# Layer 2's first products on half their channels, an operand made in two steps, and statistics moved to later slots

## The chip, the cores and the metric

The kernel runs on one core of a Trainium2 chip. The metric is the device time of one execution in microseconds, lower is better; the median of three executions before the change is 2750.5 us. One core has a matrix engine (TensorE, "PE" in the profile, with its weight loads as "PEld"), a vector engine (VectorE, "DVE"), an activation engine (ScalarE, "ACT"), a general engine (GpSimd, "POOL") and a queue for transfers (SyncE, "SP"). [...]

## What is computed

An image x of 1024 channels and 64 x 64 pixels goes through four layers, each as x + layer(groupnorm32(x)). Layer 0 mixes rows by a decay matrix. Layers 1 and 3 are products with a 1024 x 1024 matrix over the channels. Layer 2 is a selective scan:

```python
xz = silu(einsum('oc,bchw->bohw', in_proj_w, x) + in_proj_b)
x_ssm, res, gate = split(xz, 3, axis=1)
xf = silu(depthwise_conv3(x_ssm) + dw_b)
dbc = einsum('oc,bcn->bon', dbc_w, xf) + dbc_b
# dt, B, C and xf are gathered in a permuted order of pixels
y_h = selective_scan(x_h, dt, A, B_t, C_t, Dparam)
# and y is brought back to the order of the image
y = y_h * silu(gate) + res
return silu(einsum('oc,bchw->bohw', out_proj_w, y) + out_proj_b)

x = x + L0(gn(x)); x = x + L1(gn(x)); x = x + L2(gn(x)); x = x + L3(gn(x))
```

## The kernel before

**Products.** The pixels are cut in eight blocks nb of 512, taken as four pairs. The 1024 x 1024 products of layer 1 (W1) and of layer 2's x_ssm and res (WX, WR) are done on a pair at a time by a scheme of seven products for a 2 x 2 block product. `b_sets` makes a pair's operand tiles in steps: b21, b11 and b22 are normed quarters of the image (`make`, an activation on ScalarE, L921), t1 is such a quarter less b11, t2 = b22 - t1, t3 = t2 - b11, t4 = b21 - t2 (subtractions, L790). Each name has four tiles of 128 x 512, one for each k (KH = 4). t1's subtractions are on VectorE; those of t2, t3, t4 on GpSimd, except t2 in a stage's first pair and all of them in WX's last pair. A step ends at each `yield`.

`multiply` issues seven products for each half g of the output channels (NG = 2), so fourteen for a pair, in the order b21, b11, b22, t2, t3, t1, t4 (called p1 to p7 here, p8 to p14 for the second half). A product is two output tiles o times four k, eight matmuls of 128 x 512 (L835), each of which the trace shows as two records. Two pairs of accumulator banks alternate; after a product, `put` copies or adds its result and `add` adds to it (layer 1: on VectorE, L936 and L940, into the image in place; WX: `put2a` L1081 copies on ScalarE to xs and `add2a` L1089 adds on VectorE; WR: rg, L997 and L1001).

`run` goes over the pairs. While a pair is multiplied, the next pair's first five steps are taken, one after each of the last five products, and the rest (`late`) after the first products of its own pair.

**Order of the work.** Around these stages the order on PE, DVE, ACT and POOL is that in which the program writes the instructions; only SP's list is set by a planner. So what stands ahead of what is read from the code and from the trace.

**The border of layers 1 and 2.** The loop over layer 1's products takes the group norm's statistics for layer 2 in two halves of the channels: FIRST, the channels of the first half g, and SECOND. `norm_steps` turns them into a bias and a scale: a matmul over groups (pg, L198), three small vector operations (L201 to L203), a second matmul (pv, L207), and `rsqrt` with two activations and three vector operations. For FIRST (gn2a) this runs beside layer 1's last products. Behind the loop two activations make b21[0] and b21[1], whose channels are in FIRST. `multiply` with `begun` takes p1's k = 0, 1 for both outputs and then k = 2, 3; after the first half it yields, SECOND's statistics (gn2b) are finished, and five steps of the set are taken.

**With the scan (WR).** The scan over the permuted tokens goes on between half products: a gather from DRAM (L1237, on POOL), a turn on PE (pr, L1251 and L1252), decays on DVE (L1258 to L1266), pg on PE (L1273), E and its sum on DVE (L1281, L1283), G (L1286), y as a matmul with G (py, L1290), its copies on ACT (L1293, L1295) and a scatter to DRAM (L1299, on POOL). Behind WX a loop of its own (from L1211) does the last convolutions: `follow` turns finished tiles (L1057), convolves (L1035, L1038) and applies a Silu (L1109); between, half products of WR's first pair are issued.

**Gate, out_proj and layer 3** go by the same scheme on two levels, 49 slots a job (`two_steps`, matmul L1641, operands L1405 and L1409). A job of the kind "out" adds the image to its four result tiles by an accumulating DMA from GpSimd (`take_image`), takes their statistics on VectorE (`quarter_stats`, L1448) and stores the tiles (`keep`); what each needs is put on a list of slots by `on(slot, ...)`. The statistics of a pair's last tiles (Q and D) fall into the first slots of the next pair's gate job, beside the subtractions for its own operands (qt, L1405).

Of the kernel before, what the change touches and what calls it, by code (L numbers as in the profile page):

```python
# [18 lines left out]
P = 128  # L19
# [25 lines left out]
KH = CT // 2  # L45
# [45 lines left out]
def tile_net(ctx: ExitStack, tc: tile.TileContext, x, par_d, cst_d, w_d, w2_d, dbcw_d, out):  # L91
# [684 lines left out]

    def b_sets(B, make, first=False, eng=None):

        def plain(name, row, col):
            B.setdefault(name, [])  # L780
            for k in range(len(B[name]), KH):
                t = b_tile(name, k, B["name"])
                make(t, row * KH + k, col)
                B[name].append(t)

        def comb(name, one, two, ks, eng):
            if name not in B:
                B[name] = [b_tile(name, k, B["name"]) for k in range(KH)]
            for k in ks:
                eng.tensor_tensor(B[name][k], B[one][k], B[two][k], ALU.subtract)  # L790

        slow = nc.vector if first else eng or nc.gpsimd
        plain("b21", 1, 0)
        yield
        plain("b11", 0, 0)
        yield
        plain("b22", 1, 1)
        yield
        plain("t1", 0, 1)
        comb("t1", "t1", "b11", range(KH), nc.vector)  # L800
        yield
        comb("t2", "b22", "t1", range(KH), slow)
# [14 lines left out]
    def multiply(m, B, put, add, fine=False, begun=False):  # L817

        for g in range(NG):
            one, two = ("A", "B") if turn_[0] == 0 else ("B", "A")
            turn_[0] ^= 1

            def banks(tag, what):
                return [gemm[-1].tile([P, FB], F32, tag=tag, name=f"mm{what}_{m}_{B['name']}_{g}_{i}")
                        for i in range(OG)]

            def product(to, i, name, fresh):
                w = weights(m, g, i)  # L830
                split = begun and g == 0 and i == 1
                for j in range(2):
                    for o, ks in ((0, range(2 * j, 2 * j + 2)), (1, range(2 * j, 2 * j + 2))) if split else ((j, range(KH)),):
                        for k in ks:
                            nc.tensor.matmul(to[o], w[:, k, o * P : (o + 1) * P], B[name][k],  # L835
                                             start=(fresh and k == 0), stop=(k == KH - 1),
                                             skip_group_check=True)
                    if fine and j == 0:
                        yield True

            def out(fn, row, col, ps):
                for o in range(OG):
                    fn(row * KH + g * OG + o, col, ps[o])

            b = banks(two, 2)
            yield from product(b, 1, "b21", True)
            out(put, 0, 0, b)
            yield
            a = banks(one, 1)
            yield from product(a, 0, "b11", True)  # L850
            out(add, 0, 0, a)
            yield
            b = banks(two, 3)
            yield from product(b, 6, "b22", True)
            out(put, 0, 1, b)
            yield
            yield from product(a, 4, "t2", False)
            out(put, 1, 0, a)
            yield
            b = banks(two, 7)  # L860
            yield from product(b, 5, "t3", True)
            out(put, 1, 1, b)
# [11 lines left out]
    def run(pairs, mats, make, put, add, before=None, after=None, last_eng=None, fine=False, tell=False, B=None, begun=None):  # L874

        def sets(i):
            B = begun if begun and i == 0 else {"name": f"{mats[0]}_{pairs[i]}"}  # L880

            def steps():
                if before is not None:
                    before(pairs[i])
                yield from b_sets(B, lambda t, ct, col: make(t, ct, 2 * pairs[i] + col), first=(i == 0),
                                  eng=last_eng if i == len(pairs) - 1 else None)
            return B, steps()


        if B is None:  # L890
            B, steps = sets(0)
            for _ in range(5 if begun is None else 0):
                next(steps)
        else:
            steps = iter(())
        for i, pair in enumerate(pairs):
            late = steps
            nxt, steps = sets(i + 1) if i + 1 < len(pairs) else (None, iter(()))
            left = 7 * NG * len(mats)
            for m in mats:  # L900
                for half in multiply(m, B, lambda o, c, ps: put(m, o, 2 * pair + c, ps),
                                     lambda o, c, ps: add(m, o, 2 * pair + c, ps), fine, begun and i == 0):
                    if half:
                        yield True
                        if B is begun and "b11" not in B:
                            for _ in range(5):
                                next(late)
                        continue
                    if tell:
                        yield False  # L910
                    left -= 1
                    next(steps if left < 5 else late, None)
# [52 lines left out]
    with tc.manual_schedule(engines={E_.DVE, E_.PE, E_.Pool, E_.Activation}):  # L965
        for i, _ in enumerate(pointwise("l1", W1, "b1", [3, 2] + EARLY, x0_d, x1_d)):
            busy = next(sums, None) if i % 14 < 13 else None
            sort_on(not busy, (0, 0, 0, 0, 3, 2, 1, 2, 1, 3, 3, 3, 0, 0)[i % 14])
            if i == last - 6:
                chain = norm_steps("gn2a", *moments("gn2a", FIRST), len(FIRST), finer=True)  # L970
            elif last - 6 < i < last - 1:
                next(chain)
            elif i == last - 1:
                columns(FIRST, finish_of(chain), norm2)
                mv2 = moments("gn2b", SECOND, range(2))
        for _ in sums:
# [35 lines left out]
    with tc.tile_pool(name="l2a", bufs=2) as pa, tc.tile_pool(name="l2a2", bufs=1) as pa2, \  # L1012
# [68 lines left out]
            nc.scalar.copy(xs[o][:, 2 + side * FB : 2 + (side + 1) * FB], ps)  # L1081

        CONVS = 2
        have, ready, due, due2, due3 = set(), [], [], [], []

        def add2a(m, o, nb, ps):
            pair, side = divmod(nb, 2)
# [11 lines left out]
        def follow():  # L1099


            for c in due3:
                turn(*c)
            made = [conv(*c) for c in due]
            due3[:] = due2
            due2[:] = []
            for o, nb, ps in made:
                cv = pa.tile([P, FB], F32, tag="cv", name=f"cv{o}_{nb}", bufs=4)
                nc.scalar.activation(cv, ps, AF.Silu)  # L1109
                due2.append((o, nb, cv))  # L1110
            due[:] = ready[:CONVS]
            del ready[:CONVS]

        def finish(pair):
            n = 2 * TPB
# [55 lines left out]
        with tc.manual_schedule(engines={E_.DVE, E_.PE, E_.Pool, E_.Activation}):  # L1171
            nc.sync.dma_start(both[:, :, P:], dbcw_d)
            nc.gpsimd.tensor_copy(both[:, :, :P], ident.unsqueeze(1).to_broadcast([P, CT, P]))
            nc.gpsimd.memset(row, 0.0)
            ends, i = iter(()), -1
# [196 lines left out]
    def two_steps(jobs, norm2):  # L1372
# [96 lines left out]
        def plan(j):  # L1469
# [89 lines left out]
            for name, row, col, when in done:  # L1559
# [207 lines left out]
```

## Time and profile before

| what | us |
|---|---|
| median of three executions | 2750.5 (2749.68 to 2762.02) |
| profiled execution | 2756.69 |
| its span | 2754.8 |
| granted clock of TensorE, mean over the span | 0.979 |
| layer 1's last product ends, on PE | 617.57 |
| layer 2's first product begins | 620.24 |
| idle time of PE there, for b on ACT | 2.68 and 2.36 |
| idle time of PE for G at three borders of pairs of WR | 2.31, 2.34, 3.68 |
| idle time of PE for qt in three gate jobs | 1.63, 2.45, 1.95 |

In lines of the profile the first number is a start in us from the span's beginning, the second a duration, then engine, line, operation, output<-inputs, partitions x elements and the count of instructions. What stands in brackets is the engine's idle time ahead of it and the instruction that ended it. Lines of the view of waits give the waiting instruction, what it waited for, the time in all, how often, and the longest.

### The profile page before, as it was taken

To read this page: it belongs to the slowest core of one execution; us is meant where nothing else is said; L and a number is where in the kernel's file an instruction comes from. 1 tells how busy PE (TensorE), PEld (TensorE's weight loads), DVE (VectorE), ACT (ScalarE), POOL (GpSimd) and SP (SyncE) were. 2 spreads that over 40 slices of the span, in tenths; PEclk is the share of its full clock that TensorE was granted. 3 is DMA by queue.
4 is the path that set the end of the run, shared out by engine and by line. 5 is a ranking of instruction groups with operands and counts; after the bars stand their busy time and mean duration, and the time that the engine had idled before them with its cause. 6 is when DMAs were issued, how large, how long until landed. Compare 5 with 4: busy or idle time off the path is not lost.

```text
span 2754.8 us, 30917 instructions
## 1 busy us (share of the span) xinstructions
PE 2622.8 (95%) x9594; PEld 1731.6 (63%) x9594; DVE 1818.7 (66%) x3793; ACT 1090.1 (40%) x1840; POOL 1225.4 (44%) x1103
## 2 busy tenths in 40 slices
PE   4788999999999999999999999999999999999998
PEld 3664444444555555544444446888888888788887
DVE  7996766464455555476677665577576675777777
ACT  4783110104655654475657554322233133221220
POOL 4154323421213002356575654565565565555544
PEclk9898999999999999999999999999999999999999
DMA  7345467735533444688777875889899898788896
GB/s 284 113 164 189 159 220 251 233 113 194 161 106 113 130 135 94 173 249 227 225 212 219 275 208 150 240 244 295 218 287 270 242 292 232 247 285 298 296 326 217
DMA packets 423449, 591.47 MB, mean 215 GB/s; under 512 B 149973, under 2 KB 211541, under 8 KB 420214
## 3 DMA queue, kind: packets, MB, share of 16 engines
q1 hardware_dynamic: 298934, 365.76, 42.8%
q10 hardware_dynamic: 91456, 136.33, 14.0%
q0 software_dynamic: 32896, 87.40, 12.4%
q8 instruction: 78, 1.28, 0.2%
q14 instruction: 85, 0.70, 0.1%
HBM read 432.02 MB, written 157.36 MB: 214 GB/s over the span
## 4 chain that ended last, share of the span: by engine, by line
PE 44%; POOL 5%; DMA 5%; issue 3%; DVE 2%; ACT 1%; SPq 0%; POOLq 0%; DVEq 0%; ACTq 0%
PE mm L835 8%; PE q_P6P L1641 5%; PE q_P3P L1641 5%; PE q_P7P L1641 5%; PE q_P2P L1641 4%; PE q_P5P L1641 4%; PE q_P4P L1641 4%; PE q_P1P L1641 4%; DMA y_d<-y,dst 2%; DMA qD<-x_d 2%; POOL s L461 1%; PE py L1290 1%; PE pg L1273 1%; DMA g<-tok_d,src 1%; POOL t_b L1405 1%
## 5 line engine op out<-in xcount | busy, mean ns | idle before, releaser
L835 PE MATMUL mm<-t,w 128*128 128x512 f32 x1536 | 684.1, 596 | 0.5 <-DVE image L936 0.5
L835 PE MATMUL mm<-b,w 128*128 128x512 f32 x1152 | 519.6, 603 | 7.4 <-ACT b L921 7.4
L835 PEld LDWEIGHTS mm<-t,w 128*128 128x128 f32 x1536 | 286.9, 191 | 328.0 <-issue 321.8
L835 PEld LDWEIGHTS mm<-b,w 128*128 128x128 f32 x1152 | 218.4, 193 | 261.1 <-issue 246.8
L1299 POOL DMA_INDIRECT y_d<-y,dst x74 | 73.6, 994 | 193.9 <-ACT y L1295 108.7
L1038 DVE SCALAR_TENSOR_TENSOR cvp<-xs,par,cvp 128x512 f32<-128x512 f32 x128 | 95.3, 753 | 82.8 <-ACT cvp L1035 80.5
L1610 ACT COPY qQ<-q_P5P 128x512 f32<-128x512 f32 x48 | 28.1, 585 | 291.0 <-PE q_P5P L1641 291.0
L1065 POOL TENSOR_TENSOR acc<-l2xt,acc 128x136 f32<-128x136 f32 x56 | 27.0, 482 | 248.3 <-ACT l2xt L1059 247.3
L461 POOL TENSOR_TENSOR s<-s 128x256 f32<-128x256 f32 (+3 forms) x120 | 129.0, 1081 | 7.9
L1293 ACT COPY g<-py 8x512 f32<-8x512 f32 x146 | 83.8, 574 | 122.3 <-PE py L1290 118.3
L790 POOL TENSOR_TENSOR t<-b,t 128x512 f32<-128x512 f32 x72 | 94.4, 1341 | 55.7 <-DVE t L790 31.5
L1089 DVE TENSOR_TENSOR xs<-mm,xs 128x512 f32<-128x512 f32 x64 | 41.6, 684 | 114.9 <-PE mm L835 114.9
L936 DVE SCALAR_TENSOR_TENSOR image<-mm,par,image 128x512 f32<-128x512 f32 x64 | 47.1, 746 | 105.0 <-PE mm L835 104.9
L1281 DVE TENSOR_TENSOR E<-E,pg 128x512 f32<-128x512 f32 x74 | 50.7, 685 | 79.1 <-PE pg L1273 74.7
L1057 PEld LDWEIGHTS l2pt<-both,cv 128*128 128x128 f32 x512 | 77.6, 192 | 35.6 <-issue 25.6
L1641 PE MATMUL q_P4P<-t_t,wq_P4P 128*128 128x256 f32 x384 | 93.8, 388 | 0.0
L1409 ACT ACTIVATE qb<-x_x_b,gn_bias,gn_r_r 128x512 f32<-128x512 f32 x64 | 48.9, 806 | 113.0 <-DMA wq_P4P<-s_d 32.3
L1405 POOL TENSOR_TENSOR t_t<-qt,t_t 128x512 f32<-128x512 f32 x46 | 69.7, 1515 | 51.9 <-DVE qt L1405 51.6
L1641 PE MATMUL q_P1P<-t_b,wq_P1P 128*128 128x256 f32 x384 | 90.6, 379 | 1.5 <-POOL t_b L1405 1.5
L1641 PE MATMUL q_P2P<-t_b,wq_P2P 128*128 128x256 f32 x384 | 92.0, 383 | 0.0
L921 ACT ACTIVATE b<-image,gnl_bias,gnl_r_r 128x512 f32<-128x512 f32 x48 | 36.8, 808 | 138.0 <-PE mm L835 110.6
L1405 POOL TENSOR_TENSOR t_t<-qt 128x512 f32<-128x512 f32 x23 | 29.6, 1287 | 138.5 <-DVE qt L1405 78.4
(415 smaller groups left out, 6019.9 us busy)
## 6 DMA issues: line engine op xcount, KB each, us to landing
w<-s_d SPq DMA_DIRECT2D x96, 512.0 KB
w<-in_w_dram SPq DMA_DIRECT2D x72, 512.0 KB
x_x_b<-x_d ACTq DMA_DIRECT2D x28, 1024.0 KB
image<-x_d SPq DMA_DIRECT2D x12, 2048.0 KB
wq_P6P<-s_d SPq DMA_DIRECT2D x84, 256.0 KB
wq_P7P<-s_d SPq DMA_DIRECT2D x84, 256.0 KB
wq_P5P<-s_d SPq DMA_DIRECT2D x84, 256.0 KB
wq_P3P<-s_d SPq DMA_DIRECT2D x84, 256.0 KB
```

The lines of the kernel that those rows point to most:

```text
L461: eng.tensor_tensor(out, a, b, ALU.subtract)
L790: eng.tensor_tensor(B[name][k], B[one][k], B[two][k], ALU.subtract)
L835: nc.tensor.matmul(to[o], w[:, k, o * P : (o + 1) * P], B[name][k], start=(fresh and k == 0), stop=(k == KH - 1), skip_group_check=True)
L936: nc.vector.scalar_tensor_tensor(part, ps, pcol(bias_name, o), part, ALU.add, ALU.add)
L1038: nc.vector.scalar_tensor_tensor(cv, xo[:, at + t : at + t + FB], pcol("dww", 3 * o + t), cv, ALU.mult, ALU.add)
L1057: nc.tensor.matmul(pt[:, q * NV : (q + 1) * NV], cv[:, (q0 + q) * P : (q0 + q + 1) * P], both[:, o, :], start=True, stop=True)
L1281: nc.vector.tensor_tensor(Ef, Ef, pg, ALU.mult)
L1293: nc.scalar.copy(rows[k + 1][h * LC : h * LC + S, :DH], py[h * LC : h * LC + S])
L1299: nc.gpsimd.indirect_dma_start(out=y_d[:, :], out_offset=bass.IndirectOffsetOnAxis(ap=dst_[:, k : k + 1], axis=0), in_=y[:, :], in_offset= ...
L1405: eng.tensor_tensor(to, a, b, ALU.subtract)
L1409: nc.scalar.activation(tile_of(j, name)[:, k], held[j, "x", name][:, k], AF.Identity, bias=bias, scale=scale)
L1641: nc.tensor.matmul(ps[:, o, :], w[:, k, o * P : (o + 1) * P], rhs[:, k, :], start=(new and o == 0 and k == 0), stop=(k == 1), skip_group_c ...
```

## The change

There are four parts. (1) Layer 2's first two products begin with k = 0, 1: b21[0], b21[1], b11[0] and b11[1] are made in the loop's last step but one, ahead of the last products' additions and of the two stores of the image. PE takes b21's k = 0, 1, then gn2b_pg, b11's k = 0, 1 for the first output, gn2b_pv, b11's k = 0, 1 for the second, then the other halves. SECOND's norm is taken in three turns between these. (2) `b_sets` makes t1 in two steps of two tiles each, so that a set has ten steps. (3) The Silu of convolved tiles is written in a function of its own, `follow_on`, which in the loop behind WX is called after half a product. (4) The statistics of the "out" jobs other than the final one come 10 slots after their tile in place of 7, and the store 11 in place of 8 behind the last. The number of matmuls and transfers stays.

```diff
-        def plain(name, row, col):
+        def plain(name, row, col, upto=KH):
             B.setdefault(name, [])
-            for k in range(len(B[name]), KH):
+            for k in range(len(B[name]), upto):
...
-        plain("t1", 0, 1)
-        comb("t1", "t1", "b11", range(KH), nc.vector)
-        yield
+        for upto in (2, KH):
+            plain("t1", 0, 1, upto)
+            comb("t1", "t1", "b11", range(upto - 2, upto), nc.vector)
+            yield
...
+            def some(to, w, name, fresh, o, ks=range(KH)):
+                for k in ks:
+                    nc.tensor.matmul(to[o], w[:, k, o * P : (o + 1) * P], B[name][k],
+                                     start=(fresh and k == 0), stop=(k == KH - 1), skip_group_check=True)
...
-            b = banks(two, 2)
-            yield from product(b, 1, "b21", True)
-            out(put, 0, 0, b)
-            yield
-            a = banks(one, 1)
-            yield from product(a, 0, "b11", True)
-            out(add, 0, 0, a)
-            yield
+            b = banks(two, 2)
+            if begun and g == 0:
+                a = banks(one, 1)
+                wb, wa = weights(m, g, 1), weights(m, g, 0)
+                for to, w, name, o, then in ((b, wb, "b21", 0, None), (b, wb, "b21", 1, True),
+                                             (a, wa, "b11", 0, True), (a, wa, "b11", 1, "rest")):
+                    some(to, w, name, True, o, range(2))
+                    if then:
+                        yield then
+                for to, w, name, fn in ((b, wb, "b21", put), (a, wa, "b11", add)):
+                    for o in range(OG):
+                        some(to, w, name, True, o, range(2, KH))
+                    out(fn, 0, 0, to)
+                    yield
+            else:
...
-                        if B is begun and "b11" not in B:
+                        if half == "rest":
                             for _ in range(5):
                                 next(late)
...
             elif i == last - 1:
                 columns(FIRST, finish_of(chain), norm2)
                 mv2 = moments("gn2b", SECOND, range(2))
+                name = f"{WX}_{EARLY[0]}"
+                begun = {"name": name, **{b: [b_tile(b, k, name) for k in range(2)] for b in ("b21", "b11")}}
+                for b, row in (("b21", 1), ("b11", 0)):
+                    for k in range(2):
+                        normed(norm2)(begun[b][k], row * KH + k, 2 * EARLY[0])
         for _ in sums:
             pass
-        begun = {"name": f"{WX}_{EARLY[0]}", "b21": [b_tile("b21", k, f"{WX}_{EARLY[0]}") for k in range(2)]}
-        for k in range(2):
-            normed(norm2)(begun["b21"][k], KH + k, 2 * EARLY[0])
...
-            made = [conv(*c) for c in due]
+            made[:] = [conv(*c) for c in due]
             due3[:] = due2
             due2[:] = []
+            due[:] = ready[:CONVS]
+            del ready[:CONVS]
+
+        def follow_on():
             for o, nb, ps in made:
                 cv = pa.tile([P, FB], F32, tag="cv", name=f"cv{o}_{nb}", bufs=4)
                 nc.scalar.activation(cv, ps, AF.Silu)
                 due2.append((o, nb, cv))
-            due[:] = ready[:CONVS]
-            del ready[:CONVS]
+            made[:] = []
...
-                    moments("gn2b", SECOND, range(2, 4), mv2)
                     n = len(SECOND)
-                    columns(SECOND, finish_of(norm_steps("gn2b", mv2[:, 0, :n], mv2[:, 1, :n], n)), norm2)
+                    if chain is None:
+                        moments("gn2b", SECOND, range(2, 4), mv2)
+                        chain = norm_steps("gn2b", mv2[:, 0, :n], mv2[:, 1, :n], n, finer=True)
+                        turns = 0
+                    turns += 1
+                    if turns < 3:
+                        next(chain), next(chain)
+                    else:
+                        columns(SECOND, finish_of(chain), norm2)
...
                     follow()
+                    follow_on()
...
                 follow()
-                for _ in range(2):
-                    next_units(6)
+                next_units(6)
+                follow_on()
+                next_units(6)
                 activate(len(silus))
...
                         for i in range(2):
-                            on(when[k + 1] + 7 + i, lambda name=name, row=row, nb=nb, k=k + i: quarter_stats(
+                            on(when[k + 1] + 10 + i, lambda name=name, row=row, nb=nb, k=k + i: quarter_stats(
                                 tile_of(j, name), row, nb, k))
-                    end += 8
+                    end += 11
```

More of the change, by code (lines that the diff above doesn't have):

```diff
@@ L827, in banks @@
                         for i in range(OG)]
+            def some(to, w, name, fresh, o, ks=range(KH)):
+                for k in ks:
+                    nc.tensor.matmul(to[o], w[:, k, o * P : (o + 1) * P], B[name][k],
+                                     start=(fresh and k == 0), stop=(k == KH - 1), skip_group_check=True)
             def product(to, i, name, fresh):
                 w = weights(m, g, i)
[L831 to L838, printed above, removed]
+                for o in range(OG):
+                    some(to, w, name, fresh, o)
+                    if fine and o == 0:
                         yield True
@@ L845, in multiply @@
             b = banks(two, 2)
-            yield from product(b, 1, "b21", True)
-            out(put, 0, 0, b)
-            yield
-            a = banks(one, 1)
-            yield from product(a, 0, "b11", True)
-            out(add, 0, 0, a)
-            yield
+            if begun and g == 0:
[7 more added lines that the diff above has]
+                for to, w, name, fn in ((b, wb, "b21", put), (a, wa, "b11", add)):
+                    for o in range(OG):
+                        some(to, w, name, True, o, range(2, KH))
+                    out(fn, 0, 0, to)
+                    yield
+            else:
+                yield from product(b, 1, "b21", True)
+                out(put, 0, 0, b)
+                yield
+                a = banks(one, 1)
+                yield from product(a, 0, "b11", True)
+                out(add, 0, 0, a)
+                yield
             b = banks(two, 3)
@@ L1083, in tile_net @@
         CONVS = 2
-        have, ready, due, due2, due3 = set(), [], [], [], []
+        have, ready, due, due2, due3, made = set(), [], [], [], [], []
         def add2a(m, o, nb, ps):
@@ L1174, in tile_net @@
             nc.gpsimd.memset(row, 0.0)
-            ends, i = iter(()), -1
+            ends, i, chain = iter(()), -1, None
             for half in run(EARLY + LATE, [WX], normed(norm2), put2a, add2a, before2,
```

## The prediction

> **What bounds the kernel now.** I began with the page's busy shares and slices, because they say whether one engine carries the span.
>
> ```profile
> PE 2622.8 (95%) x9594; PEld 1731.6 (63%) x9594; DVE 1818.7 (66%) x3793; ACT 1090.1 (40%) x1840; POOL 1225.4 (44%) x1103
> PE   4788999999999999999999999999999999999998
> PEclk9898999999999999999999999999999999999999
> ```
>
> TensorE is busy for 95% of 2754.8 us, and from slice 6 on in every slice. No other engine is near its limit, and the change keeps the matmuls' number. So only two things can move: the 132 us in which PE is idle, and the short stretches at a lower clock behind such idleness. The view of PE's waits says what the idleness is. I keep its rows that the change can reach:
>
> ```profile
> PE gn_pg L198 <- DVE gn_mv L181: 36.1, 6, 22.6
> PE py L1290 <- DVE G L1286: 9.1, 6, 3.7
> PE mm L835 <- ACT b L921: 7.4, 3, 2.7
> PE q_P6P L1641 <- DVE qt L1405: 6.0, 3, 2.5
> PE pr L1251 <- DMA g<-tok_d,src: 6.0, 5, 2.4
> PE l2pt L1057 <- ACT l2xt L1059: 4.1, 1, 4.1
> PE mm L835 <- DVE image L936: 0.5, 1, 0.5
> ```
>
> (Columns: us in all, times, longest.) Of the first row 32.4 us lie in the span's first 210 us, in layer 0, which the change doesn't touch. The reader is to see how small the rest is: the third, second, fourth and last rows sum to 23.0 us.
>
> PE's timeline then shows these waits in place. At the border of layers 1 and 2:
>
> ```profile
> 620.24 5.13 PE L835 MATMUL mm<-b,w 128*128 128x512 f32 x8 [2.68 <-ACT b L921]
> 626.13 0.38 PE L207 MATMUL gn2b_pv<-gn2b_d,cst 128*128 128x4 f32 x2 [0.64 <-DVE gn2b_d L203]
> 628.88 19.13 PE L835 MATMUL mm<-b,w 128*128 128x512 f32 x40 [2.36 <-ACT b L921]
> ```
>
> Eight records take 5.13 us here, and 3.65 us in the scan's stage (below). The bracket is idle time and the longer row is the clock: each wait is paid twice. Between pairs of the scan's stage (third case, PE then DVE):
>
> ```profile
> 1509.33 3.65 PE L835 MATMUL mm<-t,w 128*128 128x512 f32 x8
> 1516.66 1.27 PE L1290 MATMUL py<-g,G 128*128 128x512 f32 x2 [3.68 <-DVE G L1286]
> 1510.52 3.84 DVE L790 TENSOR_TENSOR t<-t,b 128x512 f32<-128x512 f32 x4
> ```
>
> And in the gate's product (PE, then DVE):
>
> ```profile
> 2056.88 2.93 PE L1641 MATMUL q_P6P<-qt,wq_P6P 128*128 128x256 f32 x6 [2.45 <-DVE qt L1405]
> 2055.54 0.69 DVE L1448 BATCH_NORM_STATS2 stats<-qD 128x6 f32<-128x512 f32 x1 [3.28 <-DMA qD<-x_d]
> 2056.15 0.68 DVE L1405 TENSOR_TENSOR qt<-qb,qb 128x512 f32<-128x512 f32 x1
> ```
>
> VectorE stands 3.28 us at a statistic whose tile a DMA still fills; the operand that PE needs is the instruction behind it.
>
> [...] from 1516.66 to the next pr at 1523.58 are 6.92 us, and the same row of instructions takes 5.21 in full clock, so 1.71 too many. [...] waits of 1.95 to 3.68 us are followed by slow records, those up to 1.90 are not. [...] four subtractions took 2.48 us at 1210.60 and 3.84 at 1510.52, where a 1.14 and three 1.3 us additions ran on GpSimd.
>
> **The change, part by part.**
>
> *Layer 2's begin.* Before, layer 1's last product ends at 617.57, and ScalarE begins the first operand only behind two stores at 618.33 (it starts at 619.38). Now four activations for channels of the first half are put ahead of those. They wait for gn2a's bias, on DVE at 615.28, so they run from 615.5 to 618.4 (four at 0.72), and PE goes on at 617.57: 8 records of 0.43 for b21 (to 621.0), gn2b_pg (to 621.5), 4 of b11 (623.15), gn2b_pv (623.6), 4 of b11 (625.3). The chain behind gn2b_pv takes 1.88 us to the activations (626.13 to 628.01) and 0.87 more to PE (628.88), so b21's other half starts at 625.9 after 0.6 us of idleness, too short for the slow clock by the list above; it ends at 629.35, b11 at 632.8. ScalarE needs 12 further activations of 0.705 for b21, b11, b22 and t1, to 633.5; the copies that empty the first product's banks lie behind them (to 634.6), and p3 may begin at 634.1, as soon as its bank is free. Before, p3 began at 628.88 + 24 x 0.43 + 1.76 (slow clock) = 640.96. Gain 6.9 us. What is late next: t2, which on DVE follows t1 (ends 634.9) and needs 2.6 to 4.6 us more, 637.5 to 639.5, against p4 at 640.97. It holds by 1.5 us; bounds of this part 4.5 to 8.
>
> *T1 in two steps.* A set now takes ten steps, so outside the first one t1's second half goes behind the old pair's last product, t2 behind the new pair's first one and t3 and t4 one product later each. In layer 1 the 0.5 us at L936 goes (p1's additions are now ahead of t2 on DVE). In layer 2's first stage PE has no wait between pairs, and the later tiles are still early by 3 us or more (t2 ready at 744.5 for p4 at 760; t3 763.8 for 769.2; t4 782 for 785.3): nothing. With the scan, the burst ahead of G at the three borders of pairs falls from four subtractions to two. It was 2.48, 2.48 and 3.84 us and becomes 1.24 each (two of 0.62), so the waits of 2.31, 2.34 and 3.68 become about 1.1: 5.1 us. At about 1.1 us the slow clock goes as well, which measured 1.72, 1.71 and 1.71: 5.1 more. The other two subtractions now stand ahead of the next exp-and-G on DVE, where about 0.3 us each is uncovered: -0.9. Together 9.3. One thing lies against it: on GpSimd's queue t4's last two subtractions (1.34 us each) come ahead of a scatter and a gather near 1585, whose gather PE already awaited for 1.90 us. That costs between 0 (if the scatters' transfers set the time) and 2.7 plus 1.7 for the clock; I take 1.5. Bounds of the whole: 0 to 10.
>
> *Later statistics beside the gate.* They move three slots (of some 1.73 us each), in all three pairs. The transfers landed at 1876.6, 2055.5 and 2235.6; in the second case the moved statistic comes up at about 2056 to 2057, a margin of 1 us, and the subtraction for PE is ahead of it (it would run at about 2050 to 2052 where 2054.4 is needed). The waits of 1.63, 2.45 and 1.95 go: 6.0. Of the clock, 0.1, 1.71 and 1.78 go: 3.5. Together 9.5; as the margin is thin I take 1.0 off for a rest that reaches PE. The store of the D tile goes three slots later, and its buffer is asked for again some ten slots after that: free. Bounds 3 to 9.5.
>
> *Convolved tiles' activation.* In the loop behind layer 2's first stage the Silu is written behind half a product instead of ahead of it. That half emits matmuls alone. ScalarE's, VectorE's and PE's own orders stay what they were, instruction by instruction, and the 4.1 us of L1057 stay: 0.
>
> On SyncE's queue an image load and some x0_x_b loads move behind three to five weight loads; the images were loaded over a pair (some 100 us) ahead of their use: 0.
>
> Sum: 6.9 + 0.5 + 9.3 - 1.5 + 9.5 - 1.0 = 23.7 us off the profiled execution's 2756.69 (span 2754.8 and 1.9 around it): 2733. That execution is 6.2 us above the median of the runs, 2750.5; nothing in the change touches that difference, so the forecast is 2750.5 - 23.7, about **2727 us**.
>
> **Rivals.** A measurement of this kernel tells about 0.5%, 13.8 us, from no change.
>
> *One of the two larger gains fails.* Either G waits for something else in the scan's stage (the gathers; PE's fifth row is 6.0 us of them), or the statistics still meet an unfinished DMA at the later slot. For it: both margins are near 1 us. Against it: the bursts and stalls removed stand directly ahead of the late instruction. 2750.5 - 23.7 + 7.8 or + 8.5: 2735 to 2736.
>
> *Only the border of layers 1 and 2 gains:* 2750.5 - 7.4 = 2743. For it: both margins at once.
>
> *Slower: GpSimd's queue.* With the scan, gathers and scatters share GpSimd's queue with t2, t3 and t4, which now come a product later and so beside other gathers. Eight subtractions (10.7 us) of t3 and t4, moved in front of gathers that have 5.4 to 8 us from issue to use, could let PE wait twice a pair. It decides from the point where a gather is issued over 2 us later than now. Five us and 1.7 of clock, two times, in three pairs are 40 us: 2767. Against it: GpSimd is busy for 44% only, and its queue keeps the order of all but a few of the gathers.
>
> *It doesn't do what it says.* For the fourth part that is my reading; for the rest the instructions do move.
>
> **How the numbers follow.** My forecast 0.50; one gain fails 0.28; border only 0.12; slower 0.10. The forecast's case counts as faster; of the second, whose times lie 2 us under the bound of 2736.7, three quarters count as faster and the rest as no change; the third is no change: faster 0.71, same 0.19, slower 0.10. Range: parts at their better ends give 8 + 0.5 + 10 + 9.5 = 28 and 2722, a little lower if the slow clock goes elsewhere too; above it takes in the first two rivals: 2720 to 2746.
>
> **What would show it.** Right: no "mm L835 <- ACT b L921" over 1 us and p3 near 634; py's waits for G near 1.1 us with eight records in 3.65 behind them; no wait of q_P6P for qt; L1057's wait still there. Wrong: new waits of PE for g, for t on GpSimd or for t2 behind the border, or statistics that still end a DMA wait of 3 us ahead of qt.

## The result, and the profile after

The changed kernel takes 2735.98 us in the median of five executions (2732.57 to 2736.82), the kernel before 2750.50 beside it. The ratio is 0.9935, 95% interval [0.9914, 0.9955]. With 2750.5 that is 17.9 us less (12.4 to 23.7); the medians alone differ by 14.5 us. The forecast was 2727 (23.7 us less), with a range of 2720 to 2746. A second set on another chip gave 2735.86 and 0.9932 [0.9914, 0.9950]. So it became faster as forecast, by about three quarters of the forecast amount. One execution of the variant e4 below ran at a granted clock of 0.861 and took 3043.76 us; it is left out of that variant's median and ratio.

To see where, I cut both profiled executions at the same instructions on PE: layer 1's first product, its end, p4 of layer 2's first pair, the scan's first pr, the gate's first q_P1P, and the end. The view of windows gives each stretch (start:end), its length, and then the busy time of PE, PEld, DVE, ACT and POOL, PE's granted clock, the transfers' share and GB/s. Three of the six stretches, before:

```profile
224.69:617.57 392.88, 390.24 (x908) 171.96 (x908) 242.37 (x657) 49.95 (x69) 133.29 (x94) 0.99 0.57 187
...
1132.79:1674.89 542.10, 524.67 (x1401) 250.35 (x1400) 375.72 (x814) 328.69 (x565) 305.55 (x310) 0.99 0.76 222
1674.89:2754.80 1079.91, 1056.66 (x4968) 924.33 (x4968) 751.86 (x1047) 283.56 (x438) 607.41 (x450) 0.99 0.86 262
```

After:

```profile
222.48:619.86 397.38, 391.78 (x908) 172.68 (x909) 237.32 (x657) 52.19 (x72) 133.52 (x94) 0.99 0.55 185
...
1127.15:1665.15 538.00, 522.20 (x1402) 248.76 (x1400) 375.32 (x814) 328.07 (x565) 306.67 (x311) 0.99 0.76 224
1665.15:2735.00 1069.85, 1054.13 (x4968) 923.47 (x4968) 750.16 (x1047) 283.69 (x438) 604.77 (x450) 0.99 0.85 264
```

| stretch | before | after | difference | forecast |
|---|---|---|---|---|
| layer 0, not touched | 224.69 | 222.48 | -2.2 | 0 |
| layer 1 | 392.88 | 397.38 | **+4.5** | -0.5 |
| its end to p4 of layer 2 (617.57 to 647.84; 619.86 to 643.07) | 30.27 | 23.21 | -7.1 | -6.9 |
| rest of WX | 484.95 | 484.08 | -0.9 | 0 |
| scan, WR | 542.10 | 538.00 | **-4.1** | -7.8 |
| gate, out_proj, layer 3 | 1079.91 | 1069.85 | -10.1 | -8.5 |

The rows sum to -19.9 (rounded), the spans differ by 19.8. The 2.2 us of layer 0 are chance (the same kernel in e5 has 224.81 there), which leaves 17.6 for the change, near the 17.9 of the ratio. Three rows are near the forecast. Layer 1 became longer, and the scan's stage gained half of what it should.

Of PE's waits after, the rows that bear on the change:

```profile
PE pr L1280 <- DMA g<-tok_d,src: 7.6, 5, 2.8
...
PE py L1319 <- DVE G L1315: 5.6, 8, 1.2
...
PE l2pt L1074 <- ACT l2xt L1076: 4.1, 1, 4.1
PE mm L832 <- POOL t L790: 4.0, 1, 4.0
PE mm L832 <- ACT b L936: 2.9, 2, 2.4
...
PE q_P6P L1670 <- DVE qt L1434: 0.3, 1, 0.3
```

G's waits fell from 9.1 to 5.6 with 1.2 the longest, qt's from 6.0 to 0.3, and the activations' from 7.4 to 2.9 (2.4 of it at the start of layer 1, as before). l2pt's 4.1 stands. New is the row for t on POOL, and the first, for the gathers, grew from 6.0. The third border, at which the prediction shows 3.68:

```profile
1503.44 1.10 PE L1319 MATMUL py<-g,G 128*128 128x512 f32 x2 [1.15 <-DVE G L1315]
```

The eight matmul records behind it (from 1505.24) take 3.60 us, at a granted clock of 1.00.

At the border of layers 1 and 2, PE's timeline goes as the prediction laid it out:

```profile
619.86 3.60 PE L832 MATMUL mm<-b,w 128*128 128x512 f32 x8
...
627.88 7.13 PE L832 MATMUL mm<-b,w 128*128 128x512 f32 x16 [0.54 <-ACT b L936]
636.10 7.13 PE L832 MATMUL mm<-b,w 128*128 128x512 f32 x16 [1.09 <-ACT xs L1098]
```

The first product follows layer 1 without idleness and in full clock (eight records in 3.60 us at a granted clock of 1.00, where they took 5.13 at 0.71), and waits of 0.54 (0.6 was forecast) and 1.09 (1.3) remain. p3 starts 16.2 us behind layer 1's end; 16.5 was forecast.

### The profile page after: what moved, and what is told of

Its sections match the earlier page's. It is cut to its first block, busy times and chain, and to the rows that moved or that the text cites. A ratio compares the mean times of both kernels' runs of the same rounds, so it can differ in the third digit from the quotient of the medians.

```text
span 2735.0 us, 30900 instructions
## 1 busy us (share of the span) xinstructions
PE 2613.8 (96%) x9594; PEld 1726.7 (63%) x9594; DVE 1804.5 (66%) x3793; ACT 1089.8 (40%) x1840; POOL 1224.4 (45%) x1103
## 3 DMA queue, kind: packets, MB, share of 16 engines
q10 hardware_dynamic: 91456, 136.33, 14.2%
q8 instruction: 78, 1.28, 0.2%
## 4 chain that ended last, share of the span: by engine, by line
PE 47%; DMA 4%; POOL 3%; issue 3%; DVE 2%; ACT 1%; SPq 0%; POOLq 0%; DVEq 0%; ACTq 0%
PE mm L832 8%; PE q_P6P L1670 5%; PE q_P5P L1670 5%; PE q_P7P L1670 5%; PE q_P2P L1670 5%; PE q_P4P L1670 5%; PE q_P3P L1670 5%; PE q_P1P L1670 5%; DMA y_d<-y,dst 2%; PE py L1319 1%; POOL s L461 1%; PE pg L1302 1%; POOL t L790 1%; DMA g<-tok_d,src 0%; PE pr L1280 0%
## 5 line engine op out<-in xcount | busy, mean ns | idle before, releaser
L936 ACT ACTIVATE b<-image,gnl_bias,gnl_r_r 128x512 f32<-128x512 f32 x48 | 37.2, 809 | 138.1 <-PE mm L832 111.5
L1670 PE MATMUL q_P5P<-t_t,wq_P5P 128*128 128x256 f32 x384 | 90.8, 379 | 0.0
L1670 PE MATMUL q_P6P<-t_t,wq_P6P 128*128 128x256 f32 x384 | 90.7, 379 | 0.0
L1670 PE MATMUL q_P7P<-t_t,wq_P7P 128*128 128x256 f32 x384 | 90.7, 379 | 0.0
```

Source lines behind the costliest of these rows:

```text
L1670: nc.tensor.matmul(ps[:, o, :], w[:, k, o * P : (o + 1) * P], rhs[:, k, :], start=(new and o == 0 and k == 0), stop=(k == 1), skip_group_c ...
```

## The experiments

### Each part alone

*e1.* The kernel before with part one alone: the three edits of `multiply`, of `run` and of layer 1's loop, and `b_sets` as before.

> The kernel before with the first part of the change alone (layer 2's begin on half the channels). From the two traces, the stretch from layer 1's last product to p3 went from 23.4 to 16.2 us. If that gain is kept to the end, this is 7 us faster than before, about 2743.5 against 2750.5 (ratio 0.9974), with p3 about 16 us behind layer 1's last product. Rival: the next stage takes it back at its own pace (its operands come from one loop over engines), and the time stays within 2 us of before.

Measured: 2745.02 beside 2750.22, ratio 0.9982 [0.9974, 0.9989], so 5.0 us less (3.0 to 7.2). The gain is kept; the rival, that the time stays within 2 us of before, falls. In its trace p4 comes 7 us earlier relative to layer 1's end, as in the changed kernel.

*e2.* The kernel before with part two alone.

```diff
-        plain("t1", 0, 1)
-        comb("t1", "t1", "b11", range(KH), nc.vector)
-        yield
+        for upto in (2, KH):
+            plain("t1", 0, 1, upto)
+            comb("t1", "t1", "b11", range(upto - 2, upto), nc.vector)
+            yield
```

> The kernel before with the second part alone (t1 in two steps). By the traces this part brings a wait of some 4 us for t4 on GpSimd in layer 1 (behind a weight sum that waits for a DMA) and 2 us of clock behind it, takes about 7.7 us off at the three borders of pairs with the scan, and loses some 4 to 5 us of that to gathers at the end: net between -3 and +3 us, 2747.5 to 2753.5 (ratio 0.999 to 1.001). Rival, my prediction's sum for this part: -8.3 us, 2742. If the wait for t4 in layer 1 belongs to another part, it isn't in this trace.

Measured: 2751.71, ratio 1.0007 [1.0001, 1.0014], so 0.3 to 3.9 us slower. The part that I had put at -8.3 us gains nothing here. Its trace has the new wait of layer 1:

```profile
468.16 7.09 PE L836 MATMUL mm<-t,w 128*128 128x512 f32 x12 [4.10 <-POOL t L790]
```

p7 stops after a quarter of its sixteen records, at t4's third tile. GpSimd's timeline shows why. Before the change:

```profile
431.38 4.96 POOL L790 TENSOR_TENSOR t<-b,t 128x512 f32<-128x512 f32 x4
465.92 1.27 POOL L470 TENSOR_TENSOR s<-s 128x512 f32<-128x512 f32 x1 [29.59 <-DMA s<-in_w_dram]
```

In the changed kernel, in which PE's wait for t4 ends at 465.88:

```profile
459.43 1.27 POOL L470 TENSOR_TENSOR s<-s 128x512 f32<-128x512 f32 x1 [27.43 <-DMA s<-in_w_dram]
460.77 3.83 POOL L461 TENSOR_TENSOR s<-s 128x512 f32<-128x512 f32 x3
464.57 2.48 POOL L790 TENSOR_TENSOR t<-b,t 128x512 f32<-128x512 f32 x2
```

GpSimd waits 27.43 us for a weight block from DRAM, adds it up, and only then takes t4's last two subtractions. Before the change all four of t4 ran at 431.38, ahead of that wait. One product later in the program put two of them behind it, and in these traces GpSimd doesn't take them ahead of the waiting addition (they begin at 464.57, behind its end). Ahead of this place the changed kernel's PE is 2.40 us earlier than before's, behind it 3.83 us later: 6.2 us lost, of which 4.0 is the wait and 2.0 clock (twelve records take 7.20 us from 465.88 to 473.08, at a granted clock of 0.76, and 5.15 from 614.71 to 619.86, at 1.00). A wait of 1.18 us for the sort, which then had time, went, and gave 1.4 back.

*e3.* The kernel before with part four alone (7 to 10 and 8 to 11).

> The kernel before with the fourth part alone (statistics three slots later). If the stall at the statistic is the whole cause, the three waits of q_P6P for qt are gone and the time is 9 to 10 us less: 2741 (ratio 0.9965). Rival: before's profiled execution, 6 us above the median, showed longer stalls than most executions have, and the median gains only 3 to 6 us: 2745 to 2747.

Measured: 2743.27, ratio 0.9973 [0.9961, 0.9984], so 4.4 to 10.7 us less. q_P6P has no wait for qt in its trace, and the gate's stage is 10.2 us shorter there. The rival with 3 to 6 us isn't excluded by the interval; the waits for qt do vary from one trace to the next (6.0 in sum in before, and 6.7, 5.1 and 7.4 in e1, e2 and e8, which have this part as before).

*e4.* The changed kernel with t1 in one step.

> The changed kernel with t1 in one step again (parts one, three and four stay). If the second part's net worth is about zero, as the traces say, this stands within 3 us of the changed kernel's 2736: 2733 to 2739, with the wait for t4 in layer 1 gone and the three long waits for G back. If the second part is worth what the prediction said (-8.3), it is 2744.

Measured: 2738.20, ratio 0.9952 [0.9939, 0.9965]. The wait for t4 in layer 1 is gone, and G is awaited for 2.3 and 3.7 us again (the third such wait, 2.4 us, is put down to a copy ahead of it). The prediction's 2744 falls. The changed kernel is 2.2 us below this by the medians and 4.7 by the ratios, and the intervals overlap.

*e8.* The kernel before with part three alone (`follow_on` as in the change, and called as here; in the other place it is called right behind `follow`).

```diff
                 follow()
-                for _ in range(2):
-                    next_units(6)
+                next_units(6)
+                follow_on()
+                next_units(6)
```

> The kernel before with the third part alone (Silu of convolved tiles written behind half a product). The order on each engine is that of before, so 0.999 to 1.001 of before, with PE's 4.1 us wait at the turn (l2pt) still there. Rival: the wait is shorter, and the time 2 to 4 us less.

Measured: 2747.83 beside 2753.08, ratio 0.9990 [0.9976, 1.0004]. No difference that can be told, and the wait of l2pt is 4.11 us in its trace as in that of before.

### What the split of t1 costs

*e5* is the changed kernel once more, beside the next two.

> The changed kernel once more, on the same chip as the three beside it, to compare with them. Expected 0.9935 to 0.996 of before, with the wait for t4 in layer 1 (about 4 us) and the gathers' waits at the end of the scan's stage again if they belong to the order of instructions; if they were chance of one execution, they are gone or elsewhere.

Measured: 2735.86, ratio 0.9932 [0.9914, 0.9950]. The wait for t4 (4.3) and those for the gathers (1.9, 2.7, 0.6, 1.1 in the last pair of WR) are there again, so they belong to the order of instructions.

*e6.* The split only in the sets of WR.

```diff
-        for upto in (2, KH):
+        cuts = (0, 2, KH) if B["name"].startswith(f"{WR}_") else (0, KH)
+        for lo, upto in zip(cuts, cuts[1:]):
             plain("t1", 0, 1, upto)
-            comb("t1", "t1", "b11", range(upto - 2, upto), nc.vector)
+            comb("t1", "t1", "b11", range(lo, upto), nc.vector)
             yield
```

> The changed kernel with t1 in two steps only in the sets of WR (beside the scan), one step in layer 1 and WX. If the wait for t4 behind the weight sum on GpSimd is what the split costs in layer 1, it goes, and this is 5 to 6 us faster than the changed kernel (ratio to before lower by 0.002). Rival: the weight sum's DMA is what sets the time there, and the wait comes up at a neighbouring instruction: no difference.

Measured: 2731.95 and again, as e9, 2734.57; ratios 0.9925 [0.9907, 0.9943] and 0.9940 [0.9928, 0.9952]. The trace has the predicted event: the wait for t4 is gone and PE gains 6.2 us on the changed kernel there; 2 us go back to the sort's wait, so layer 1 is 3.7 us shorter. The time doesn't show the 5 to 6 us expected, and the intervals don't part it from the changed kernel. In its trace the scan's stage is 1.8 us longer than in the changed kernel's (a gather is awaited for 1.50 us at 1269.13 instead of 0.59), and layer 0 2.5 us longer by chance.

*e7.* All sets with nine steps: t1's second half in the step of t2.

```diff
-        for upto in (2, KH):
-            plain("t1", 0, 1, upto)
-            comb("t1", "t1", "b11", range(upto - 2, upto), nc.vector)
-            yield
+        plain("t1", 0, 1, 2)
+        comb("t1", "t1", "b11", range(2), nc.vector)
+        yield
+        plain("t1", 0, 1)
+        comb("t1", "t1", "b11", range(2, KH), nc.vector)
```

> The changed kernel with t1 made two and two tiles, but the second two in the same step as t2, so that a set keeps nine steps and t3 and t4 stand where they stood before the change. My theory: the G waits stay near 1.1 us as in the changed kernel, and both costs of the split go, the wait for t4 in layer 1 (6 us with its clock) and most of the gathers' 5 us at the end of the scan's stage: 8 to 11 us faster than the changed kernel, about 2726. Rival: the gathers are bound by the transfers themselves, and only layer 1's 5 to 6 us come back. Second rival: t2 on GpSimd now waits for the later half of t1 and holds up the gather behind it, so that this is slower than the variant with the split in the scan only.

Measured: 2733.12, ratio 0.9927 [0.9910, 0.9944]. My theory's 2726 falls. Layer 1's wait is gone, but G is late a second time at two borders, by 2.05 and 2.35 us. VectorE's timeline in e7, and then in the changed kernel, at the same place:

```profile
1362.84 3.08 DVE L790 TENSOR_TENSOR t<-t,b 128x512 f32<-128x512 f32 x2
```

```profile
1362.86 1.28 DVE L790 TENSOR_TENSOR t<-t,b 128x512 f32<-128x512 f32 x2
```

The same two subtractions take 3.08 us instead of 1.28; GpSimd's first two of t2 run from 1362.27 on in e7 (2.49 us), and none of them beside it in the changed kernel. That is 0.9 us more for each subtraction beside GpSimd's. At the third border it is the same (3.38 us for two). In this way the burst that the split took away from G came back. GpSimd itself waited for t1's later half for only 0.64 us, so the second rival is right in that t2 is now too near to t1, and wrong in how.

### What makes the gathers late

In the changed kernel's last pair of WR, GpSimd and then PE:

```profile
1559.27 0.97 POOL L1266 DMA_INDIRECT g<-tok_d,src  x1 [0.30 <-issue]
...
1571.28 3.56 POOL L461 TENSOR_TENSOR s<-s 128x448 f32<-128x448 f32 x3
1574.79 2.51 POOL L790 TENSOR_TENSOR t<-b,t 128x512 f32<-128x512 f32 x2
1577.45 1.00 POOL L1328 DMA_INDIRECT y_d<-y,dst  x1
1578.75 0.96 POOL L1266 DMA_INDIRECT g<-tok_d,src  x1 [0.30 <-issue]
```

```profile
1564.83 0.55 PE L1280 MATMUL pr<-cst,g 128*112 128x192 f32 x2 [2.81 <-DMA g<-tok_d,src]
1584.72 0.55 PE L1280 MATMUL pr<-cst,g 128*112 128x192 f32 x2 [2.58 <-DMA g<-tok_d,src]
1592.12 0.55 PE L1280 MATMUL pr<-cst,g 128*112 128x192 f32 x2 [1.41 <-DMA g<-tok_d,src]
1592.74 5.35 PE L832 MATMUL mm<-b,w 128*128 128x512 f32 x8
```

The three waits are those for the gathers issued at 1559.27, 1578.75 and 1585.27. Ahead of the second, t4's last two subtractions lie between the weight sum and the scatter, where there were none before the change, and the gather lands 5.97 us after its issue (1578.75 to 1584.72). Before, PE waited at the same place too:

```profile
1593.47 0.55 PE L1251 MATMUL pr<-cst,g 128*112 128x192 f32 x2 [1.90 <-DMA g<-tok_d,src]
```

and for 2.41 us at the next one, while the first of the three, which lies ahead of those subtractions, had no wait (at 1576.07).

*e10.* On e6, the last pair's last two subtractions of t4 on VectorE.

```diff
+                end = B["name"] == f"{WR}_{EARLY[1]}" and (name, ks[0]) == ("t4", 2)
-                comb(name, one, two, ks, eng or nc.gpsimd)
+                comb(name, one, two, ks, nc.vector if end else eng or nc.gpsimd)
```

> The variant with t1 split beside the scan only, once more, on the chip of the three below, to compare with them. Expected about 0.9925 of before, with gathers awaited near the end of the scan's stage three times (2 to 3 us, 2 to 3 us, 1 us).

> The variant with the split beside the scan only, and in the last pair of WR the last two subtractions of t4 on VectorE in place of GpSimd. If those 2.5 us ahead of a scatter and a gather are what lets PE wait for the gather near 1587, that wait (2.6 to 3.7 us in the runs with the split) goes or falls under 1 us, and the scan's stage is 3 to 5 us shorter, since the clock behind it stays up; the wait near 1566 stays. Rival: the gather comes late because of the scatters' transfers, and the wait stays over 2 us. What could take it back: 1.2 us more on VectorE ahead of one G, a new wait of up to 1 us.

Measured on one chip: e9 2734.57 (2733.46 to 2735.51), e10 2730.24 (2728.80 to 2736.16); ratios 0.9940 [0.9928, 0.9952] and 0.9931 [0.9917, 0.9945]. In the traces e10's scan stage is 5.0 us shorter (from 0.78 to 5.78 us ahead of e9). Of these, 1.7 are there already at the end of the first of these waits (1561.78), for a gather that was issued (1556.50) before the moved subtractions ran (1558.81), so they aren't the edit's; 3.4 come after it. The wait at the second place fell from 3.45 (2.90 in e6, the same kernel) to 2.04, not below 1, and the one at 1613.19 (0.55) went:

```profile
1581.15 0.55 PE L1282 MATMUL pr<-cst,g 128*112 128x192 f32 x2 [2.04 <-DMA g<-tok_d,src]
1581.78 3.65 PE L834 MATMUL mm<-t,w 128*128 128x512 f32 x8
```

By the mark set (under 1 us) the expectation fails, and by its own (over 2 us) the rival just holds. Without t4 there, this wait is about what it was before the change (1.90), so t4's place is a part of the cause; the rest was there before, and the wait at the first place isn't touched by this edit (2.01).

*e11 and e12.* On e6 (e12: on e10), one more call of the weight sums in each fourth chunk.

```diff
                 if given // 2 % 14 != 12:
                     next(sums, None)
+                if k % 4 == 0:
+                    next(sums, None)
```

> The variant with the split beside the scan only, and the weight sums on GpSimd beside the scan called once more in each fourth chunk, so that they end about a fifth earlier (before 1560 instead of at 1637) and the last pair's gathers find GpSimd free. If GpSimd's queue makes the gathers late, the three waits of the last pair shrink to under 1 us each and the stage is 5 to 8 us shorter. Rivals: the same waits come up earlier, where the sums now are denser (no gain); or the gathers' own transfers set the time (waits stay, no gain).

> Both of the two edits above on the variant with the split beside the scan only. If both act on one cause, GpSimd's queue in the last pair, this is about equal to the better of the two; if their waits are independent, 1 to 3 us better than that. In the best case 2723 to 2726, about 0.990 of before.

Measured: 2766.70 and 2766.01, ratios 1.0061 [1.0048, 1.0075] and 1.0057 [1.0042, 1.0071], about 32 us slower than e9 beside them; the gains expected of both fall. In e11's trace the last pair's waits did fall (e9's 2.63, 3.45 and 0.55 to none over 0.4), as expected if GpSimd's queue makes them: the weight sums end at 1559.52 there, and t4's subtractions are still on GpSimd (from 1595.02). But PE waits for gathers ten times instead of five, 24.2 us instead of 8.2, earlier in the stage. GpSimd ahead of the longest of them, and then PE:

```profile
1231.68 3.55 POOL L461 TENSOR_TENSOR s<-s 128x448 f32<-128x448 f32 x3
1235.19 4.96 POOL L790 TENSOR_TENSOR t<-b,t 128x512 f32<-128x512 f32 x4
...
1241.61 0.96 POOL L1267 DMA_INDIRECT g<-tok_d,src  x1 [0.30 <-issue]
```

```profile
1248.33 0.95 PE L1281 MATMUL pr<-cst,g 128*112 128x192 f32 x2 [7.19 <-DMA g<-tok_d,src]
```

A sum and t2 back to back hold GpSimd for 8.5 us; the gather behind them is issued half a microsecond after PE could have used its data, and lands 6.7 us later. This is the mechanism of the prediction's slower rival, a gather issued too late behind other work on GpSimd, brought about here by another edit. It costs 30.5 us in the scan's stage (568.8 against 538.3, with ten waits), where the rival was given 40. The changed kernel has few such waits and stays far from that.

e10 has the lowest median of all, 4.3 us under e9 on one chip; its interval doesn't part it from e9 or from the changed kernel.

## Why the prediction was right, and where it was off

The traces of all fourteen runs, cut at the same instructions, tell which of the differences are steady:

| stretch | without the part that bears on it | with it |
|---|---|---|
| layer 1 (t4 a product later) | 391.1 to 393.7, eleven traces | 396.0 to 397.4, three |
| its end to p4 of layer 2 (part one) | 27.2 to 30.3, four | 23.2, ten |
| scan (t1 split, ten steps; e7, e11, e12 left out) | 537.1 to 542.4, median 542.3, five | 536.3 to 539.8, median 538.0, five |
| gate, out_proj, layer 3 (part four) | 1075.2 to 1082.9, four | 1068.5 to 1069.9, ten |

So layer 1's loss and the gains of parts one and four stand; in the scan's stage one trace without the split (e1, 537.1) is as short as those with it.

**Layer 2's begin: right.** Forecast -6.9 us, measured -7.1 in the trace and -5.0 (-3.0 to -7.2) alone. The two small waits came at the named places. That 7.1 is so near is partly luck: before's profiled execution has the longest of the four old stretches, and against e8's, whose waits are the same (2.68 and 2.36 us) without slow clock behind them (a stretch of 27.2 us, with eight records in 3.70 behind the first wait), the gain is 4.0.

**Statistics beside the gate: right.** Forecast -8.5, measured -10.1 in the trace and -7.4 (-4.4 to -10.7) alone. Of the 1.0 allowed for the thin margin, 0.3 us of waiting for qt came, in another job (at 2493.57).

**Convolved tiles' activation: right.** 0 was forecast, e8 shows no difference, and the 4.1 us wait is left.

**G's waits at the borders of pairs: right in kind, a little too large.** All three long waits became 1.11 to 1.15 and lost their slow clock (eight records in 3.60 us behind each, at a granted clock of 1.00). From pr to the G behind the border PE gained 1.5, 2.5 and 3.7 us by alignment of the two traces, 7.7 in sum against 9.3. The term that was too large is the one for t1's second half ahead of the next G: 0.3 a border was put down, and the first border has a new wait of 1.23 there and the others 0.26.

**Gathers: term too small, and in another place.** I took 1.5 out of bounds of 0 to 4.4 for t4's subtractions ahead of a scatter and a gather near 1585. There the cost is small: PE waits 2.58 us for 1.90 before, and at the next gather 1.41 for 2.41. In the last pair PE's lead over before shrank from 14.5 us (at the pr behind the last border) to 9.7 (at 1592.12), and nearly all of these 4.8 us went at the wait of 2.81 us at 1564.83 and the slow clock behind it (eight records in 5.35 us, at a granted clock of 0.68), ten us ahead of t4's last subtractions. PE had come there 14.2 us earlier than in before, but GpSimd issued that gather only 10.8 us earlier (1559.27 against 1570.07): what PE gained at G's borders, GpSimd didn't gain in full. By e11 the weight sums in GpSimd's queue have a part in the last pair's waits, since they go with the sums; what keeps GpSimd back at 1559 isn't settled.

**T1 in two steps in layer 1: wrong.** This is the step that failed: "In layer 1 the 0.5 us at L936 goes", with nothing set against it. For WX the prediction compares when t2, t3 and t4 are ready with when they are needed; for layer 1 it makes no such comparison and doesn't ask what else stands in GpSimd's queue. A weight sum that waits 27 us for a DMA is there, and being one product later means being behind it: 6.2 us lost, 1.4 of it returned by the sort. Even the 0.5 us at L936 is there again (0.49). e2, e4 and e6 show the cause: the wait comes with the split and goes with it.

With these terms put right (+4.5 for -0.5, 7.7 for 9.3, 4.8 for 1.5, and the small differences elsewhere), the sum is that of the trace, 17.6. The second part as a whole, a third of the forecast gain, is worth nothing that can be told: -8.3 forecast, between 0.3 and 3.9 us slower alone (e2), and beside the other parts 2 to 5 us faster, within the noise (e4). In the traces some 4 us lost in layer 1 stand against some 4 gained in the scan's stage. The slower rival named the right queue, but in the scan's stage, where its cost stayed small, and not in layer 1.

The measured 2736 is also the number that the prediction gave to its rival in which one of the two larger gains fails. That rival came true in part only. G's waits and qt's shrank as forecast; the gathers took back about half of what the scan should gain, and layer 1 lost 4.5 us, which no case of the prediction has. So the number's agreement with that rival is partly chance.

That the profiled executions differ by 19.8 us and the medians by 14.5 comes from the executions chosen: before ran from 2749.6 to 2762.0 in five, and its profiled one was 6.2 above the median. The prediction says that nothing in the change touches that difference. This is doubtful: in the 48 executions of before beside e1 to e4 the time goes with the granted clock (correlation -0.82; the fastest, 2744.45 us, had 0.984, the slowest, 2757.72, had 0.979), and about 12 of the forecast 23.7 us were slow records behind waits, taken as the profiled execution had them (3.3 at the begin, 5.1 at G, 3.5 at qt). By this an execution with less slow clock would have less to gain; that it makes up the whole difference isn't shown.

## What to carry to other kernels

If work is moved later on an engine, look first at what it is moved behind. Here a weight sum of 5.1 us on GpSimd waited 27.4 us for its transfer, the two subtractions behind it ran only after it, and 6.2 us of that reached PE; a slack worked out from busy times doesn't show it.

A short wait of the engine that sets the time cost nearly twice its length in some places here (before: 1.95 us for qt at 2236.95 and 1.78 of slow clock behind it, at a granted clock of 0.66), but the second half of that isn't paid in every execution (2.68 us in before and in e8, with eight records in 5.13 us behind it and in 3.70). What a stall on another engine cost went by what stood behind it: of VectorE's 3.28 us at a statistic before the change, 2.45 came up as PE's wait for qt, and of GpSimd's 27.43 us, 4.01 as PE's wait for t4. The gains beside the scan and beside the gate both came from taking a stalled or bulky instruction out from ahead of one that was awaited.

Splitting the burst helped the instruction behind its first half (the longest wait for G fell from 3.68 to 1.15 us at the third border) and burdened the one behind its second (the new wait of 1.23 us for G at the first border); in e7 the second half, beside GpSimd's subtractions, took longer (3.08 us) than the whole burst had at that border before (2.48).

## What the runs showed of the hardware

In these runs the length of a wait alone doesn't tell whether the slower matmul clock follows. Layer 2's first product, begun as before the change, shows it at one and the same instruction. In before's trace eight records took 5.13 us behind a wait of 2.68 (at 620.24, in the prediction; granted clock 0.71), and in e8 3.70:

```profile
620.19 3.70 PE L835 MATMUL mm<-b,w 128*128 128x512 f32 x8 [2.68 <-ACT b L921]
```

In e2 they took 5.40 and in e3 3.70, both behind 2.67. In the changed kernel 2.58 us (at 1584.72) were followed by eight records in 3.65 us, at a granted clock of 1.00, and 1.41 (at 1592.12) by eight in 5.35, at 0.67; in e10 2.04 us (at 1581.15) were followed by eight in 3.65 and 2.01 (at 1561.78) by eight in 5.35. In the prediction I read out of before's trace that each wait is paid twice, with a threshold between 1.90 and 1.95 us; neither holds. Layer 0 of before's own trace has waits of 1.82 us with eight records of 128x128 in 1.97 us behind each (1.04 in full clock at 64.80), at a granted clock of 0.50 from 207 to 217. What decides it these runs don't show. Where the slow clock came behind a wait in the scan's stage it cost about 1.7 us (5.35 against 3.65 at 1565.45 and 1592.74 in the changed kernel, 6.92 against 5.21 at 1516.66 in before).

A subtraction of one 128x512 tile from another took VectorE 0.64 us with nothing on GpSimd beside it (two in 1.28, the changed kernel at 1362.86) and 1.54 beside GpSimd's subtractions (two in 3.08, e7 at 1362.84). A gather's data reached PE 5.6 to 6.9 us after its issue in the places followed here (1559.27 to 1564.83 and 1585.27 to 1592.12 in the changed kernel, 1574.35 to 1581.15 in e10).
